# A rewritten constants block, turning of adjacency rows spread into the first run-up, and other buffers for turned rows in a four-layer graph kernel

## The chip, the core and the metric

One core of a Trainium2 chip runs the whole program. The metric is the device time of one execution in microseconds (us). The engines are TensorE (PE, with its weight loads as PEld), VectorE (DVE), ScalarE (ACT), GpSimd (POOL) and SyncE (SP). Each runs its instructions in the order in which the compiled program has them, and they meet through semaphores. All data transfers of this kernel are issued on SP's queue, in order too.

## What is computed

The inputs are `x` (16 elements of 1024 nodes with 64 features), `adj` (16 matrices of 1024 x 1024, zeros and ones) and a node mask. Four layers follow one another, each `x = x + layer(relu(layernorm(x)), adj)`:

```python
# layer 0: thin the neighbour lists, then a weighted sum of quantiles over the neighbours, then an MLP
nb = (adj_ > 0) & (~eye)[None]
m = nb.sum(-1)
rank = jnp.cumsum(nb, axis=-1) - 1
skip = jnp.where(m > T_THRESH, (m + K_DIL - 1) // K_DIL, 1)
removed = nb & do_dil[..., None] & ((rank + 1) % skip[..., None] == 0)
rem = removed | jnp.swapaxes(removed, 1, 2)
...
sv = jnp.sort(vals, axis=2)          # per node and feature, over its valid neighbours
# for tau in 0.25, 0.5, 0.75: linear interpolation between two sorted values, weights 0.25, 0.5, 0.25
out = x + agg
y = relu(out @ W1 + b1) @ W2 + b2
# layer 1: (adj + I) @ h / row sum
# layer 2: attention with 8 heads, a gate from x, and adj added to the logits
# layer 3: adj @ (h @ W3) + b3
```

Layers 1 and 3 multiply by `adj` with the contraction over its columns, so TensorE needs each block of 128 rows of `adj` turned (transposed).

## The kernel before, in words

**Order.** Two generators are interleaved at build time by the loop at the end of the function. `picks()` walks through layer 0; each of its yields hands out an amount of "due" work. `layers()` does all else: first `turned()`, which turns every block of rows of every element, and then, for each element whose layer 0 is done, `rest(b)` (layers 1, 2, 3). Each piece of `layers()` yields its own cost, and the loop lets it go on while something is due. A comparison step of `picks()` yields 0.42 (there are 96 in an element: 8 feature groups, 2 halves of the nodes, 6 order statistics); one turned block costs 0.3; the layers 1 to 3 of one element cost 40.3 together, as much as 96 steps hand out. If the next element's layer 0 isn't done yet, `layers()` yields `None` and what is due is dropped. When `picks()` has ended, `alone` is set and the rest of `layers()` runs without a partner. From the order so written a scheduler in the compiler makes the instruction order of each engine; buffers of one tag are handed out in the written order.

**Constants.** The block from L127 to L352 builds selection matrices and columns on VectorE: identities, bit-reversed indices (`bits_reversed`, `rev`), `at_row` columns, six `sel_q`. It uses a scratch pool that is closed at L389; the main pool `sb` then takes the same memory, so its first load (L394, the node mask) waits for the scratch pool's last user.

**Run-up of element 0.** `ranked(0)` loads and normalises two elements, turns them (`sv`, L956) and stores them (`h_d`). `ranks()` sorts all 1024 values of each of 128 columns in 55 steps of a bitonic network (L577 to L579, three VectorE instructions each), storing the choices (`md`), and stores the sorted values (`vs_d`); then it reads the choices back (`sb`, L597) and runs the 55 steps in reverse on an index row (`rev_d`), four VectorE instructions each (L609 to L612). The result is turned on TensorE (`pr`, L619), copied by ScalarE (`rs`, L622), stored (`rk_d`) and loaded per element (`rk`, L1021). `dilate(0)`, beside it, thins the adjacency in 8 blocks (a scan on VectorE, an Abs on ScalarE, two stores). `background()` deals the two out, two steps of ranking to one of thinning. In the kernel before each of these yields hands out 0.0, so nothing else is interleaved.

**Stages of layer 0.** `stages(el)` loads `rk`, forms the neighbour masks (`neighbours`: two loads `lr` of blocks, TensorE, a ScalarE activation `valid`, 16 times), counts them (`m`, L640), makes the positions of the order statistics (`kq`, six `krow`), and the table of sorted values (`sorted_table`: `u`, `df`, `tab`). For element 0 all of it is written behind `background(0)`; for later elements it lies in the last twelve steps of the element before. `prepare` then makes weights from the ranks (`e`, L705; `cw`), `make` the rank sums (`px`, `cum`, `c1`, `c0`), and `compare` starts with `le` (L819).

**Turning.** `turned()` loads a block of rows (`ad`, L467, three buffers, shared with `dilate` and layer 2), sums it on ScalarE, turns it with eight transposes in two PSUM tiles (`pcols`, L459; copies L462) and stores it (`adjT`, L1096). `turned_rows()` (L1099 to L1102) loads a turned block for layers 1 and 3 into the tag `bt`, which has two buffers. Layer 0's `cum`, `c1` and `c0` use the tag `tb`, six buffers of the same size, which `chunk_cols` already takes for layer 2 once `alone` is set. `weighted()` multiplies a turned block (`two`, L1077), copies it through ScalarE (L1084), and adds its halves on TensorE (`po`, L1086); once alone, both PSUM tiles share one tag of two buffers.

The loop that interleaves:

```python
two, due = layers(), 0.0
for r in picks():
    due += r
    while due > 0.0:
        due -= next(two) or due
alone.append(True)
for _ in two:
    pass
```

Of the kernel before, what the change touches and what calls it, by code (L numbers as in the profile page):

```python
# [8 lines left out]
F32 = mybir.dt.float32  # L9
# [29 lines left out]
def tile_preln_adj_stack(  # L39
# [87 lines left out]
    scr_i = sc("scr_i", (P, 5, P), I32)  # L127
    scr_f = sc("scr_f", (P, 3, P))
    identf = const.tile([P, P], F32, name="identf")
    make_identity(nc, identf)  # L130
    ident = const.tile([P, P], HP, name="ident")
    nc.vector.tensor_copy(ident, identf)

    rev_i = sc("rev_i", (P, C), I32)
    nc.gpsimd.iota(rev_i, pattern=[[1, C]], base=0, channel_multiplier=C)
    rev_a = sc("rev_a", (P, C), I32)
    rev_b = sc("rev_b", (P, C), I32)
    nc.vector.memset(rev_a, 0)
    for b_ in range(N.bit_length() - 1):
        up = N.bit_length() - 2 - 2 * b_  # L140
        nc.vector.tensor_scalar(
            rev_b, rev_i, 1 << b_, abs(up), op0=OP.bitwise_and,
            op1=OP.logical_shift_left if up >= 0 else OP.logical_shift_right,
        )
        nc.vector.tensor_tensor(rev_a, rev_a, rev_b, OP.bitwise_or)
    rev = sc("rev", (P, C), HP)
    nc.vector.tensor_copy(rev, rev_a)
    rev_d = dram.tile([P, C], HP, name="rev_d")
    nc.sync.dma_start(rev_d, rev)
    minus_i = const.tile([P, P], BF, name="minus_i")  # L150
    nc.vector.tensor_scalar(minus_i, identf, -1.0, None, op0=OP.mult)
# [3 lines left out]
    fmp_i = scr_i[:, 0, :]  # L155
    nc.gpsimd.iota(fmp_i, pattern=[[1, P]], base=0, channel_multiplier=-1)
    fmp = scr_f[:, 0, :]
    nc.vector.tensor_copy(fmp, fmp_i)


    step2 = sc("step2")
    nc.vector.scalar_tensor_tensor(step2, fmp, 2.0, identf, op0=OP.is_equal, op1=OP.subtract)
    dif = const.tile([P, 2, P], HP, name="dif")
    nc.vector.tensor_scalar(dif[:, 0, :], step2, -SPAN, None, op0=OP.mult)
    nc.vector.tensor_scalar(dif[:, 1, :], step2, -1.0, None, op0=OP.mult)
    less = const.tile([P, 2, P], HP, name="less")
    nc.vector.tensor_scalar(less[:, 0, :], identf, -2.0, None, op0=OP.mult)
    nc.vector.tensor_scalar(less[:, 1, :], identf, -FINE, None, op0=OP.mult)

    prow_i = scr_i[:, 1, :]  # L170
    nc.gpsimd.iota(prow_i, pattern=[[0, P]], base=0, channel_multiplier=1)
    fcol_i = scr_i[:, 2, :]
    nc.gpsimd.iota(fcol_i, pattern=[[1, P]], base=0, channel_multiplier=0)
    par_i = scr_i[:, 3, :]


    sel_w = const.tile([P, 2, 2 * BKW], HP, name="sel_w")
    nc.vector.tensor_scalar(par_i, prow_i, 1, None, op0=OP.bitwise_and)
    par = const.tile([P, 2], F32, name="par")
    nc.vector.tensor_copy(par[:, 1:2], par_i[:, 0:1])  # L180
    nc.vector.tensor_scalar(par[:, 0:1], par[:, 1:2], -1.0, 1.0, op0=OP.mult, op1=OP.add)
    par_up = const.tile([P, 2], F32, name="par_up")
    nc.vector.tensor_scalar(par_up, par, UP, None, op0=OP.mult)
    for c2 in range(2):
        cols = slice(c2 * BKW, (c2 + 1) * BKW)
        for i, w in enumerate((2.0, 2.0 * FINE)):
            nc.vector.tensor_scalar(
                sel_w[:, i, cols], fcol_i[:, :BKW], 0.0, w, op0=OP.mult, op1=OP.add
            )
            nc.vector.tensor_scalar(sel_w[:, i, cols], sel_w[:, i, cols], par[:, c2 : c2 + 1], None, op0=OP.mult)  # L190

    def bits_reversed(x, bits, n, name):
        r, u = sc(name + "_r", (P, n), I32), sc(name + "_u", (P, n), I32)
        nc.vector.memset(r, 0)
        for i in range(bits):
            up = bits - 1 - 2 * i
            nc.vector.tensor_scalar(
                u, x, 1 << i, abs(up), op0=OP.bitwise_and,
                op1=OP.logical_shift_left if up >= 0 else OP.logical_shift_right,
            )  # L200
            nc.vector.tensor_tensor(r, r, u, OP.bitwise_or)
        return r


    pblk = scr_i[:, 3, :]
    same = scr_f[:, 1, :]
    fblk = scr_i[:, 4, :]
    nc.vector.tensor_scalar(fblk, fcol_i, 4, None, op0=OP.logical_shift_right)
    fpl = sc("fpl", (P, P), I32)
    nc.vector.tensor_scalar(fpl, fcol_i, 15, None, op0=OP.bitwise_and)  # L210
    fplr = bits_reversed(fpl, 4, P, "fpl")
    ppl = sc("ppl", (P, P), I32)
    nc.vector.tensor_scalar(ppl, prow_i, 15, None, op0=OP.bitwise_and)
    pplr = bits_reversed(ppl, 4, P, "ppl")
    nc.vector.tensor_scalar(pblk, prow_i, 4, None, op0=OP.logical_shift_right)
    nc.vector.tensor_tensor(same, pblk, fblk, OP.is_equal)

    to30 = const.tile([P, 2], I32, name="to30")
    field = sc("field", (P, P))
    nc.vector.tensor_scalar(field, pplr, 15.0, None, op0=OP.is_equal)  # L220
    keep = sc("keep", (P, P))
    nc.vector.tensor_scalar(keep, field, -1.0, 1.0, op0=OP.mult, op1=OP.add)
    nc.vector.tensor_scalar(to30[:, 0:1], pplr[:, 0:1], 15.0, keep[:, 0:1], op0=OP.add, op1=OP.mult)
    nc.vector.tensor_scalar(
        to30[:, 1:2], field[:, 0:1], -65536.0 - 1073741824.0, 1073741824.0, op0=OP.mult, op1=OP.add
# [3 lines left out]
    tri = scr_f[:, 2, :]  # L229
    nc.vector.tensor_tensor(tri, pplr, fplr, OP.is_le)  # L230
    nc.vector.tensor_tensor(tri, tri, same, OP.mult)
    nc.vector.tensor_scalar(tri, tri, 0.5, None, op0=OP.mult)
    nc.vector.scalar_tensor_tensor(tri, identf, -40.5, tri, op0=OP.mult, op1=OP.add)
    nc.vector.tensor_tensor(tri, tri, keep, OP.mult)
    nc.vector.tensor_tensor(field, field, same, OP.mult)
    nc.vector.scalar_tensor_tensor(tri, field, 1.0 / KHI, tri, op0=OP.mult, op1=OP.add)
    nc.vector.tensor_scalar(field, fplr, 15.0, -0.5, op0=OP.is_equal, op1=OP.mult)
    nc.vector.tensor_scalar(field, field, 1.0, None, op0=OP.add)
    nth = const.tile([P, P], BF, name="nth")
    nc.vector.tensor_tensor(nth, tri, field, OP.mult)  # L240
# [3 lines left out]
    nc.vector.memset(sel_t, 0.0)  # L244
    for i in range(2):
        nc.vector.tensor_tensor(sel_t[:, i, 8 * i : 8 * i + 8], pblk[:, 0:8], fcol_i[:, 0:8], OP.is_equal)

    sel_c = const.tile([P, 8], F32, name="sel_c")
    nc.vector.tensor_scalar(pblk, prow_i, 7, None, op0=OP.bitwise_and)
    nc.vector.tensor_tensor(sel_c, pblk[:, 0:8], fcol_i[:, 0:8], OP.is_equal)  # L250
# [3 lines left out]
    fbk = sc("fbk", (P, P), I32)  # L254
    nc.vector.tensor_scalar(fbk, fcol_i, 1, None, op0=OP.logical_shift_right)
    pbk = sc("pbk", (P, P), I32)
    nc.vector.tensor_scalar(pbk, prow_i, 63, None, op0=OP.bitwise_and)
    pbkr = bits_reversed(pbk, 6, P, "pbk")
    for e in range(2):
        nc.vector.tensor_tensor(tab_d[:, e, :], fbk, pbkr, OP.is_equal)  # L260
    nc.vector.tensor_scalar(pbkr, pbkr, 1.0, None, op0=OP.add)
    fnx = sc("fnx", (P, P))
    nc.vector.tensor_tensor(fnx, fbk, pbkr, OP.is_equal)
    nc.vector.tensor_scalar(pbk, prow_i, 6, None, op0=OP.logical_shift_right)
    for e in range(2):
        nc.vector.tensor_tensor(tab_d[:, e, :], tab_d[:, e, :], fnx, OP.subtract)
        ph_ = sc("ph_", (P, P))
        nc.vector.tensor_scalar(ph_, pbk, float(e), None, op0=OP.is_equal)
        nc.vector.tensor_tensor(tab_d[:, e, :], tab_d[:, e, :], ph_, OP.mult)
# [4 lines left out]
    nc.vector.memset(none, 0.0)  # L274
    ones = const.tile([P, P], BF, name="ones")
    nc.vector.memset(ones, 1.0)

    k16 = const.tile([P, NBK, 2], HP, name="k16")
    nc.vector.tensor_scalar(
        k16.rearrange("p b s -> p (b s)"), fbk, 16.0, 15.0, op0=OP.mult, op1=OP.add  # L280
    )

    prow = sc("prow", (P, 1))
    nc.vector.tensor_copy(prow, prow_i[:, 0:1])
    off = sc("off", (P, 2))
    bkt = sc("bkt", (P, 1), I32)
    nc.vector.tensor_scalar(bkt, prow_i[:, 0:1], 1, None, op0=OP.logical_shift_right)
    nc.vector.tensor_scalar(off[:, 0:1], bkt, 8.0, -SHIFT, op0=OP.mult, op1=OP.add)
    nc.vector.tensor_scalar(off[:, 1:2], bkt, 0.0, None, op0=OP.is_equal)
    shifts = const.tile([P, 6], F32, name="shifts")  # L290
    nc.vector.tensor_scalar(
        shifts[:, 0:1], off[:, 0:1], -1.0, None, op0=OP.mult
    )
    nc.vector.tensor_scalar(
        shifts[:, 1:2], off[:, 0:1], -SPAN, None, op0=OP.mult
    )
    first = (FIRST - SHIFT) * SPAN / FINE
    rest_ = 8.0 * SPAN / FINE
    nc.vector.tensor_scalar(
        shifts[:, 2:3], off[:, 1:2], first - rest_, rest_, op0=OP.mult, op1=OP.add  # L300
    )
    nc.vector.tensor_scalar(shifts[:, 3:4], shifts[:, 2:3], FINE, None, op0=OP.mult)
    nc.vector.memset(shifts[:, 4:5], -0.5)
    nc.vector.memset(shifts[:, 5:6], 2.0 * (160.0 - FIRST) + 2.0)

    def at_row(dst, terms):

# [203 lines left out]
    def neighbours(left_d, rem_d, t):  # L511
# [3 lines left out]
        for j in range(C):  # L515
# [22 lines left out]
            if j < C - 1:  # L538
                yield None
        yield valid  # L540

    def ranks(V):

# [775 lines left out]
```

## Time and profile before

| what | value |
|---|---|
| runs of the kernel | 12626.17 us median (12620.15 to 12635.34) |
| the profiled execution | 12620.06 us, of which the span of the instructions is 12618.3 |
| VectorE busy | 11557.3 us, 92% of the span |
| TensorE busy | 11271.0 us, 89% |
| ScalarE busy | 9465.7 us, 75% |
| GpSimd busy | 1.4 us, 10 instructions |
| data moved | 908.21 MB, 72 GB/s in the mean |

The profile is of one execution. A group of instructions is named by its line, its engine, its operation and the tiles that it writes and reads (`out<-in`), with partitions x elements. Times of the timeline count from the start of the span. Durations of neighbouring instructions on VectorE and ScalarE overlap a little, so start to start is the better measure of what one costs in a row of many. A line of waits reads: who waited, for whom, total us, how many times, the longest. Waits are inferred from semaphores: of several, the one that came last is named. An engine's share of busy time is a mean over stages that are bound by different things; the stages are therefore read one by one.

### The profile page before, as it was taken

What the parts mean: (1) busy time and instruction counts of PE and PEld (TensorE: products, weight loads), DVE (VectorE), ACT (ScalarE), POOL (GpSimd) and SP (SyncE); (2) the same over time, 40 slices, a digit from 0 to 9 for tenths busy, and PEclk for the clock granted to TensorE, in tenths of its full rate; (3) what the DMA queues carried; (4) which work ended last, traced back from release to release, by engine and by line L of the source; (5) the groups of instructions that cost most, each with busy time, mean ns of one, the idle gap of its engine ahead of it and who ended that gap; (6) DMA issues with size and microseconds to landing.
All of it is one profiled execution on the core that took longest, in us unless ns stands there. A gap on an engine that the chain in (4) does not pass through costs nothing. (4 is left out here: it accounts for less than half of the span.)

```text
span 12618.3 us, 217315 instructions
## 1 busy us (share of the span) xinstructions
PE 11271.0 (89%) x84666; PEld 5355.3 (42%) x84673; DVE 11557.3 (92%) x19682; ACT 9465.7 (75%) x17018; POOL 1.4 (0%) x10
## 2 busy tenths in 40 slices
PE   0888999999899998999989999999999999999988
PEld 0334444444444444444444444444444444444445
DVE  8899989999899999989999899999989999988873
ACT  0897877777777777777877777777777777787866
POOL 0000000000000000000000000000000000000000
PEclk9999999999999999999999999999999999999989
DMA  3672121221212122121211212112121211201011
GB/s 105 219 248 82 56 75 52 71 65 57 71 53 82 55 63 65 54 79 56 71 57 56 78 56 75 54 61 71 55 77 53 72 62 57 88 30 56 31 52 60
DMA packets 521609, 908.21 MB, mean 72 GB/s; under 512 B 240768, under 2 KB 275712, under 8 KB 520576
## 3 DMA queue, kind: packets, MB, share of 16 engines
q1 hardware_dynamic: 520576, 894.31, 21.9%
q8 instruction: 663, 10.86, 0.4%
q14 instruction: 370, 3.03, 0.1%
HBM read 683.38 MB, written 206.57 MB: 71 GB/s over the span
## 5 line engine op out<-in xcount | busy, mean ns | idle before, releaser
L821 DVE TENSOR_TENSOR wa<-le,c 128x2048 f16<-128x2048 f16 x1536 | 1868.8, 1217 | 189.4 <-PE prep L842 127.7
L735 PE MATMUL px<-valid,cw 128*128 128x512 fp8e4 x8192 | 1964.9, 381 | 0.0
L823 DVE TENSOR_TENSOR wb<-le,c 128x2048 f16<-128x2048 f16 x1536 | 1866.9, 1215 | 0.0
L819 DVE TENSOR_TENSOR le<-cum,krow 128x2048 f16<-128x2048 int16 x1536 | 1862.5, 1213 | 2.9 <-ACT cum L406 2.3
L406 ACT ACTIVATE c<-px,shifts 128x512 f16<-128x512 f32 x2048 | 1428.1, 700 | 258.4 <-PE px L762 126.1
L406 ACT ACTIVATE s<-s,nm 128x1024 f32<-128x1024 f32 x1024 | 1171.5, 1147 | 243.1 <-DVE nm L1210 230.1
L735 PEld LDWEIGHTS <-cw 128*128 128x128 f16 x8192 | 799.2, 98 | 1133.1 <-issue 240.1
L459 PE MATMUL pcols<-identf,s 128*128 128x128 f32 x8192 | 1177.8, 281 | 112.5 <-ACT eT L462 49.1
L1201 PE MATMUL sp<-kT,qT 64*128 64x512 f32 x4096 | 1163.5, 641 | 62.8 <-DVE nm L1210 61.3
L869 DVE SCALAR_TENSOR_TENSOR vs<-pz,vs 128x512 f32<-128x512 f32 x1536 | 1047.2, 682 | 148.4 <-PE pz L862 110.4
L459 PEld LDWEIGHTS pcols<-identf,s 128*128 128x128 f32 x8192 | 906.1, 142 | 641.3 <-ACT eT L462 273.4
L849 ACT COPY wi<-prep 128x512 f32<-128x512 f32 x1536 | 913.0, 594 | 347.1 <-PE prep L842 315.6
L842 PE MATMUL val<-le,tab 128*32 128x512 f16 x12288 | 1147.6, 390 | 23.6 <-ACT wi L849 13.1
L462 ACT COPY eT<-pcols 128x512 f32<-128x512 f32 x2048 | 1133.1, 603 | 26.2 <-PE pcols L459 24.8
L406 ACT ACTIVATE high<-px,shifts 128x512 f16<-128x512 f32 x1024 | 712.9, 696 | 582.4 <-PE px L735 577.4
L1224 PE MATMUL ao<-eT,v 128*64 128x128 f32 x16384 | 1071.4, 276 | 21.8 <-ACT eT L462 20.2
L406 ACT ACTIVATE vs<-val 128x512 f32<-128x512 f32 x1536 | 939.5, 612 | 192.1 <-PE val L842 117.5
L1224 PEld LDWEIGHTS ao<-eT,v 128*64 128x64 f32 x16384 | 903.8, 137 | 278.2 <-ACT eT L462 153.7
L842 PE MATMUL prep<-wb,sel_w 128*32 128x512 f16 x6144 | 664.6, 396 | 214.4 <-DVE wb L823 204.7
L1210 DVE CUSTOM_DVE_ANT_0 s<-sp,ad,nm 128x512 f32<-128x512 f32 x1024 | 725.9, 744 | 122.7 <-PE sp L1201 122.6
L857 DVE TENSOR_SCALAR bit<-wi,to 128x512 int32<-128x512 int32 x1536 | 827.0, 538 | 3.6 <-ACT cw L406 2.8
L1210 DVE CUSTOM_DVE_ANT_0 s<-sp,ad 128x512 f32<-128x512 f32 x1024 | 683.3, 682 | 121.7 <-PE sp L1201 112.3
(271 smaller groups left out, 18163.5 us busy)
## 6 DMA issues: line engine op xcount, KB each, us to landing
ad<-in_adj_dram SPq DMA_DIRECT2D x768, 512.0 KB
aT<-adjT SPq DMA_DIRECT2D x256, 512.0 KB
adjT<-aT SPq DMA_DIRECT2D x128, 512.0 KB
md<-sm SPq DMA_DIRECT2D x216, 256.0 KB
sb<-md SPq DMA_DIRECT2D x216, 256.0 KB
rem_d<-rem SPq DMA_DIRECT2D x128, 256.0 KB
left_d<-nb SPq DMA_DIRECT2D x128, 256.0 KB
lr<-left_d SPq DMA_DIRECT2D x256, 128.0 KB
```

Of the source, the lines that this page charges most:

```text
L406: nc.scalar.activation(out_, in_, func, **kw)
L459: nc.tensor.transpose(pt[:, c, :], ad[:, (4 * s + c) * P : (4 * s + c + 1) * P], identf)
L462: nc.scalar.copy(aT[:, 4 * s : 4 * s + 4, :], pt)
L735: yield nc.tensor.matmul(px[pp], w[:, j, :], valid[:, j, :], start=False, stop=j == C - 1, skip_group_check=True,)
L819: nc.vector.tensor_tensor(le, cum, bc(el.krow[q][:, None, hs], [P, 4, 512]), OP.is_lt)
L821: nc.vector.tensor_tensor(wa, le, c0, OP.mult)
L823: last = nc.vector.tensor_tensor(wb, le, c1, OP.mult)
L842: yield nc.tensor.matmul(dst[32 * pp : 32 * pp + 32, :], w[pp], r[pp], start=i == 2, stop=i in (1, 3), tile_position=(0, 32 * pp), skip_gr ...
L869: nc.vector.scalar_tensor_tensor(vs, pz, 80.0, vs, op0=OP.is_equal, op1=OP.mult)
L1201: nc.tensor.matmul(sps[e], qT[e * D : (e + 1) * D, i * P : (i + 1) * P], kT[e * D : (e + 1) * D, hs], start=True, stop=True,)
L1210: nc.vector.tensor_tensor_reduce(ss[e][:, hs], sps[e], ad[:, hs], -1.0, 3.0e38 if t == 0 else nms[e], op0=OP.add, op1=OP.min, accum_out=nm,)
L1224: nc.tensor.matmul(ao[e * D : (e + 1) * D, :], v[:, j, e * D : (e + 1) * D], eTs[e][:, j, :], start=j == 0, stop=j == C - 1, tile_position ...
```

## The change

It has four parts.

1. **Constants.** The block is written anew. Per-partition values that stood 128 wide are now columns of one element; bits of the row number are taken apart once (`ci`, `cf`, `rv`) and reused; index patterns come from more GpSimd `iota`s; copies with a scale (`ident`, `minus_i`, `less`, `dif`, `sel_q`, `mid_w`) go to ScalarE, memsets to GpSimd. The store of `rev_d` is written behind the loads of the weights.
2. **Run-up.** A yield of `background(0)` hands out 0.07 where it handed out 0.0, so `turned()` is interleaved with it. The stages of element 0 join the deal as soon as thinning has ended, beside the second half of the ranking; where they need the sorted values they wait (in the written order) until these are stored. Their tiles `vs`, `u` and `df` come from the tag `a4` for this element, from `q4` for the others.
3. **Ranks of element 0.** They are copied from PSUM straight into the place from which they are used (`own.rk`); the store `rk_d` stays for element 1, and element 0 no longer loads from it.
4. **Turned rows.** Once `alone` is set, `turned_rows()` takes `tb` with its six buffers.

```diff
+    def scaled(name, shape, dt, src, scale):
+        t = const.tile(list(shape), dt, name=name)
+        nc.scalar.activation(t, src, AF.Copy, scale=scale)
+        return t
+
+    ident = scaled("ident", (P, P), HP, identf, 1.0)
...
+    NB = 7
+    ci = sc("ci", (P, NB + 7), I32)
+    for b_ in range(NB):
         nc.vector.tensor_scalar(
-            rev_b, rev_i, 1 << b_, abs(up), op0=OP.bitwise_and,
-            op1=OP.logical_shift_left if up >= 0 else OP.logical_shift_right,
+            ci[:, b_ : b_ + 1], prow_i, b_, 1, op0=OP.logical_shift_right, op1=OP.bitwise_and
         )
...
+    rv = sc("rv", (P, NB))
+    nc.vector.tensor_copy(rv[:, 0:1], odd)
+    for b_ in range(1, NB):
+        nc.vector.scalar_tensor_tensor(
+            rv[:, b_ : b_ + 1], rv[:, b_ - 1 : b_], 2.0, cf[:, b_ : b_ + 1], op0=OP.mult, op1=OP.add
+        )
...
+    nc.vector.tensor_scalar(qs[:, 1:7], identf[:, 0:NQ], -KHI, qs[:, 0:1], op0=OP.mult, op1=OP.add)
     for q in range(NQ):
-        at_row(sel_q[:, q, :], ((q, -KHI), (R_TOP, ones_top * KHI), (R_MID, KHI)))
+        nc.scalar.activation(sel_q[:, q, :], qs[:, q + 1 : q + 2].to_broadcast([P, P]), AF.Copy)
...
-    nc.vector.memset(wproj, 0.0)
+    nc.gpsimd.memset(wproj, 0.0)
...
+    nc.sync.dma_start(rev_d, rev)
     scr.close()
...
+    def place(name):
+        return sb.tile([P, C, D], HP, tag="rk", bufs=2, name=name)
+
...
+        if own is not None:
+            own.rk = place("rk")
+            nc.scalar.copy(own.rk, pt[:, :, :D])
         rs = b2_("rs", (P, C, P), HP)
         nc.scalar.copy(rs, pt)
...
         els[0] = arrive(0)
         for r in background(0):
-            yield 0.0
+            yield 0.07
         for _ in els[0].stages:
             pass
...
             except StopIteration:
                 going.remove(gen)
+                if b == 0 and gen is thinning:
+                    going.append(els[0].stages)
                 continue
...
-        h_d, rk_d, vs_d = pairs[b // 2]
-        el.rk = sb.tile([P, C, D], HP, tag="rk", bufs=2, name="rk")
-        nc.sync.dma_start(el.rk, rk_d[:, :, rows])
-        yield
+        pair = pairs[b // 2]
+        if b:
+            el.rk = place("rk")
+            nc.sync.dma_start(el.rk, pair[2][:, :, rows])
+            yield
...
-        vs = q4("vs")
-        nc.sync.dma_start(vs[rows, :], vs_d[rows, :])
-        table = sorted_table(s, vs)
+        while not pair:
+            yield
+        mine = q4 if b else a4
+        vs = mine("vs")
+        nc.sync.dma_start(vs[rows, :], pair[1][rows, :])
+        table = sorted_table(s, vs, mine)
...
     def turned_rows(b, i, name):
-        aT = sb.tile([P, C, P], F32, tag="bt", bufs=2, name=name)
+        aT = (
+            tb(name, (P, C, P), F32) if alone
+            else sb.tile([P, C, P], F32, tag="bt", bufs=2, name=name)
+        )
         nc.sync.dma_start(aT, adjT[b][i])
         return aT
```

## The prediction

> **What bounds the kernel now.** I read the page's 40 slices first (VectorE at 8 to 9 tenths nearly everywhere, TensorE too), then the busy time by stage, since the change touches only the first element's run-up, its main loop, and the last element's tail.
>
> Busy time by stage; columns: stretch, its length, then busy time (and instructions) of TensorE, its weight loads, VectorE, ScalarE, GpSimd, the granted clock, the DMA share and GB/s.
>
> ```profile
> 24.00:43.00 19.00, 2.42 (x9) 1.75 (x9) 11.94 (x52) 5.41 (x8) 0.00 (x0) 1.00 0.50 139
> 43.00:184.00 141.00, 0.00 (x0) 0.00 (x0) 140.19 (x265) 12.64 (x14) 0.00 (x0) 1.00 0.33 114
> 184.00:287.00 103.00, 1.17 (x9) 0.98 (x10) 92.28 (x225) 0.10 (x1) 0.00 (x0) 1.00 0.27 87
> 287.00:349.00 62.00, 43.15 (x185) 19.50 (x184) 17.56 (x38) 40.77 (x69) 0.00 (x0) 0.89 0.43 115
> 349.00:980.00 631.00, 538.38 (x3730) 246.81 (x3730) 591.14 (x809) 575.77 (x1055) 0.00 (x0) 0.98 0.71 244
> ```
>
> From 43 to 287 us (ranking and thinning of element 0) VectorE alone works; TensorE is empty. From 287 to 349 the roles swap: VectorE is busy 17.56 of 62 us. The next row is element 0's main loop, where VectorE is at 94%. VectorE's waits in the 62 us (total, times, longest):
>
> ```profile
> DVE m L640 <- PE pm L637: 18.4, 1, 18.4
> DVE ve L427 <- ACT sq L406: 15.2, 1, 15.2
> DVE tab L695 <- ACT df L406: 7.5, 1, 7.5
> ```
>
> All wait for work that needed only the thinned masks or the sorted values, both on hand long before 287. Its timeline (start, duration, engine, line):
>
> ```profile
> 286.90 1.01 ACT L622 COPY rs<-pr 128x1024 f16<-128x1024 f16 x1 [119.70 <-PE pr L619]
> ...
> 318.11 0.69 DVE L705 TENSOR_TENSOR e<-k,rk 128x1024 f16<-128x1024 f16 x1
> ...
> 326.30 6.08 ACT L406 ACTIVATE krow<-pkr,shifts 128x512 int16<-128x512 f32 x10
> ...
> 349.11 1.23 DVE L819 TENSOR_TENSOR le<-cum,krow 128x2048 f16<-128x2048 int16 x1 [2.31 <-ACT cum L406]
> ```
>
> The last line is the first comparison of the main loop.
>
> Before 43 us the constants come first. Waits of the DMA queue:
>
> ```profile
> SPq L394 <- DVE q_tau L315: 11.5, 1, 11.5
> SPq L394 <- DMA rev_d<-rev: 2.8, 1, 2.8
> ```
>
> The mask load (L394), ahead of the loads of x, waits for the last constant and goes at 23.80.
>
> **The change, part by part.**
>
> *Constants.* The old block is some 240 VectorE instructions, done at 23.6 us. Counting the new code gives about 88, of which some 20 are 128 wide, plus 13 small ones on ScalarE and some 14 more on GpSimd (0.1 to 0.23 us each in the trace, done by about 5 us, all beside VectorE; the weight load behind the moved memset of wproj waits at most 1 us). What does a narrow instruction cost?
>
> ```profile
> 24.07 0.15 DVE L349 TENSOR_SCALAR rq_f<-rq_f 128x1 f32<-128x1 f32 x1
> 24.26 0.16 DVE L352 TENSOR_TENSOR w_frac<-w_frac,rq_f 128x1 f32<-128x1 f32 x1
> ```
>
> Dependent ones start 0.19 apart; independent ones (14.13, 14.20 us) 0.065. The Trainium skill, "VectorE: DVE Perf Modes", section on the TRN2 errata, says each instruction pays a fixed part (58 cycles plus its elements, at 0.96 GHz), so cutting 128 elements to 1 saves only two thirds: an estimate of 61 ns. By it 88 take 5.4 us; by the dependent row 16.7. They begin at 2.2, so the block ends at 7.6 or 18.9. Chains of different constants mix, so I take 11 us, an end at 13.2. There is a floor anyway: SP issues weight loads until 9.04, rev_d goes to 9.4, and its landing took 2.8, so L394 cannot go before 12.2. L394 moves from 23.8 to 13.2: **-10.5** (ends -5 and -11.6), carried whole to 43, because the chain behind it (landing of x, normalising, turning) is unchanged.
>
> *Hand-over.* Layer 0's stages (neighbour masks, counts, six krow tiles, the table) now go beside the ranking's second half, and the ranks come to SBUF straight from PSUM instead of through HBM. What is left between the ranking's end and the first comparison: transposes 1.03, the copy of 64 columns about 0.6, then the old stretch from the first e (318.11) to 349.11, 31.0 us, less the twelve krow activations, 7.3 us, on ScalarE, its bottleneck there. 1.9 + 31.0 - 7.3 = 26 us. The old distance is 287.2 to 349.1, 62 us: -36. VectorE's part of the stages (m 2x0.69, tab 0.69+1.23+0.69, n and nr 0.54, 0.48, 0.42, 0.42, coef 0.54) is 6.4 us, which idle time covered and which now lengthens a stretch that VectorE bounds: +6.4. Sum **-30** (ends -20 and -36, the latter if the gaps of the ranking's second half, 10.7 us, take it all in).
>
> TensorE might be quicker at the hand-over, having rows to turn before. Sixteen px matmuls took 5.15 us at 320.74, eight took 1.89 at 338.40: warm, four groups would save 2.8 us. The skill's "TensorE: Matmul & The Clock Gate", Part 1, speaks against it: an idle window of about 3.4 us puts the array at half rate. A row every 6 us leaves longer gaps, so by the rule it stays cold; I take nothing.
>
> *Turned rows in the run-up.* The run-up has 1+55+55 yields of ranking, 24 of thinning and 23 of stages: 158 x 0.07 = 11.1, 37 rows at 0.3. Each issues a load and a store of 512 KB on SP, 1.35 us of ScalarE for the row sum, two copies of 0.59, eight transposes. ScalarE and TensorE are free there; VectorE has no part in it. The data fit: in the second half 18 rows x 1.05 MB in 103 us is 183 GB/s, with the 87 of the row above and 41 for the masks 311; element 0 moves 244 at a share of 0.71, so a full share is near 344. What can be late: thinning's rem waits for ScalarE's Abs, which may stand behind a row; the stages' m, tab and krow likewise; and a row's load may stand behind SP's waits for the ranking's buffers (up to 6.8 us each), while ScalarE, which runs in order, waits for that row. The nearest row is element 0's main loop, the same mix: there rem did not wait at all, m 3.8, rev 2.8 us. With the 3.2 us that the ranking already waits for sb, say **+8**. Ends: 0, and 35 us if each of 8 Abs and 6 stage crossings waits for a whole row on ScalarE (2.5 us).
>
> *Element 0's main loop* loses 37 of 128 rows:
>
> ```profile
> L1096 SPq DMA_DIRECT2D adjT<-aT x128: 319/320/1191, 334.3 to 978.2; - x128
> ```
>
> At 0.42/0.3 = 1.4 rows a comparison, the other 91 are through by comparison 64 of 96, and the last third has none. VectorE's waits in this loop:
>
> ```profile
> DVE vs L869 <- PE pz L862: 15.8, 13, 1.9
> DVE wa L821 <- PE val L842: 7.8, 5, 3.5
> DVE wa L821 <- PE prep L842: 6.8, 6, 2.4
> ```
>
> VectorE is idle 14 us from 800 to 975 (7.7 of them in 950 to 975, where rows and next element's stages meet). Rows off TensorE and ScalarE should free most: **-10** (ends 0 and -18). Not more, since VectorE's own work remains. Layers 1 to 3 of element 0 still wait for its layer 0, so later elements keep their work.
>
> *Tail.* Turned rows of the last element get six buffers for two.
>
> ```profile
> 12592.97 1.58 PEld L1077 LDWEIGHTS two<-aT,hid 128*64 128x64 f32 x16
> ...
> 12595.98 1.58 PEld L1077 LDWEIGHTS two<-aT,hid 128*64 128x64 f32 x16
> ```
>
> Rows come 3.01 us apart, also the first two, both loaded 300 us earlier; TensorE waited 0.8 us for these loads in layer 1 and 0.4 in layer 3. The row is a chain through ScalarE and two PSUM buffers: **0** (ends +1, and -9 if an earlier load lets the order overlap 0.6 us a row).
>
> Sum: -10.5 - 30 + 8 - 10 = **-42.5**. The profiled execution took 12620.06 us (span 12618.3); it would take 12577.5. The median of the runs, 12626.17, lies 6 above it, so I predict 12584. Elements 1 to 12 repeat within about 2 us of their kind (starts of the leaving step 743 and 769 apart), so a reshuffled order is worth 5 us or so either way.
>
> **Rivals.** (A) *Partial*: the shared run-up costs its upper bound of 35 us, or rows displace stages and they pile up again: -42.5 + 27 = -15, 12611. For it: SP's in-order queue, already 70 us in waits for L597 before 352. Against: in element 0 the same mix cost VectorE 7 us. (B) *Slower*: rows held by SP's blocked fetches stall ScalarE, the masks come late, and the ranking, which shares its buffers with the masks, stops for each of the rows. It needs more than 68 us to outrun the gain with 25 to spare, 1.8 us for each of 37 rows; at the 3.2 us of the one sb wait it would be 118: +68, 12694. Against: lr loads are few (32) and VectorE's stalls on DMA total 4.2 us. (C) *More*: element 0's waits all go and the tail overlaps: -42.5 - 8 - 9 - 8 (no contention) = -67, 12559. (D) *It doesn't do it*: the stages' instructions still issue last, only constants and rows count: about -15, as A.
>
> **How the numbers follow.** Forecast 0.58, A and D together 0.22, B 0.06, C 0.14. A measurement of this kernel can tell about 0.2%, 25 us, from no change: faster means under 12601. The forecast is faster in nearly all its width, C wholly: 0.74; within, A, D and some of the forecast: 0.20; slower 0.06. The forecast's own range, from its ends, is 12566 to 12604; reaching to C and most of A gives 12556 to 12617.
>
> **What would show it.** L394 issued near 13 us; ranking starting near 32; VectorE's waits for pm and df small; first comparison near 317, not 349; 37 adjT stores before it; none after about comparison 64 of element 0; rows in the tail still 3.0 us apart. Wrong if VectorE waits on sb or lr loads by tens of us between 40 and 290, if the six krow activations still stand behind the ranking's end, or if the element starts drift by more than 5 us each.

## The result, and the profile after

| | before | after |
|---|---|---|
| median of the runs | 12626.17 us (12615.45 to 12635.34) | 12566.01 us (12562.26 to 12573.39) |
| profiled execution (span) | 12620.06 us (12618.3) | 12568.08 us (12566.3) |

The ratio is 0.9954, with a 95% interval of 0.9939 to 0.9968, a gain of 0.5%. (The five runs of the kernel before include the three of the table ahead of the prediction.) The forecast was 12584 in a range of 12556 to 12617. Between the two profiled executions lie 52.0 us, where the prediction's sum had 42.5. A single execution can lie 15 us from the median of its kernel (20 runs of one kernel below: 12590 to 12614 about 12606), so what follows is read stage by stage.

Busy time by stage of the kernel after, columns as before:

```profile
13.00:31.00 18.00, 4.30 (x18) 3.46 (x19) 9.51 (x27) 6.95 (x13) 0.00 (x0) 1.00 0.60 155
31.00:172.00 141.00, 35.42 (x149) 27.90 (x149) 140.00 (x269) 51.81 (x86) 0.00 (x0) 0.53 0.71 257
172.00:275.00 103.00, 56.42 (x262) 33.81 (x261) 87.14 (x211) 55.00 (x98) 0.00 (x0) 0.72 0.89 283
275.00:316.00 41.00, 25.21 (x107) 11.98 (x105) 25.98 (x62) 31.52 (x54) 0.00 (x0) 0.76 0.40 134
316.00:950.00 634.00, 536.39 (x3518) 221.06 (x3516) 603.61 (x828) 518.14 (x926) 0.00 (x0) 0.96 0.54 185
```

The sort takes the 141 us that it took, with VectorE at 140.00, although TensorE and ScalarE now turn rows beside it and the DMA share has gone from 0.33 to 0.71. TensorE is granted 0.53 of its clock there and is busy for 35 of the 141 us.

The timeline of after, at the points shown of before:

```profile
11.53 0.34 SPq L367 DMA_DIRECT2D mk_u<-in_nodemask_dram  x1
...
285.67 0.58 ACT L599 COPY rk<-pr 128x512 f16<-128x512 f16 x1 [2.47 <-PE pr L595]
286.29 1.30 DVE L684 TENSOR_TENSOR e<-k,rk 128x1024 f16<-128x1024 f16 x2 [1.41 <-ACT rk L599]
...
308.46 1.23 DVE L798 TENSOR_TENSOR le<-cum,krow 128x2048 f16<-128x2048 int16 x1 [0.37 <-ACT cum L379]
```

The mask load goes at 11.53, not 23.80, and the first comparison comes at 308.46, not 349.11. The krow activations are gone from the end of the run-up. VectorE's waits from 24 to 310 us:

```profile
DVE ve L400 <- ACT sq L379: 8.6, 2, 7.9
DVE sd L585 <- DMA rev<-rev_d: 4.4, 1, 4.4
DVE tab L674 <- ACT df L379: 3.2, 1, 3.2
DVE sm L553 <- ACT sv L935: 2.7, 1, 2.7
DVE sd L586 <- DMA sb<-md: 2.3, 2, 1.9
```

The wait of 18.4 for `pm` is down to 0.2, and the one for `tab` from 7.5 to 3.2. The one for `ve` does not need masks or sorted values, contrary to the prediction's reading of it: it is the normalising of the next two elements, which stands in VectorE's order there, and 7.9 of its 15.2 us remain. The wait that has grown, from 1.0 to 4.4, is for the index row `rev` at the turn of the ranking (between its sort and its reverse half). The turned rows end at 759.5 us, 39 of them stored before the first comparison:

```profile
L1081 SPq DMA_DIRECT2D adjT<-aT x128: 319/326/795, 31.6 to 759.5; - x128
```

In the tail the rows of layer 3 are 3.01 us apart, as before:

```profile
12537.65 1.98 PE L1062 MATMUL two<-aT,hid 128*64 128x128 f32 x16 [0.68 <-ACT hid L1237]
12540.05 0.69 PE L1071 MATMUL po<-ident,aoT 128*128 128x64 f32 x2 [0.42 <-ACT aoT L1069]
12540.67 1.98 PE L1062 MATMUL two<-aT,hid 128*64 128x128 f32 x16
```

The stages of the profiled executions, in us. The sort is counted to the end of its last `sm`; the "hand-over" is the distance from the ranking's end to the first comparison; the "leaving step" (`o` from `y0`) ends an element's layer 0, and its main loop with it:

| stage | before | after | difference |
|---|---|---|---|
| ranking starts at | 42.82 | 29.77 | -13.05 |
| sort | 142.88 | 143.01 | +0.1 |
| turn, from the sort to the reverse half | 2.23 | 5.58 | +3.35 |
| reverse half | 98.18 | 106.51 | +8.3 |
| hand-over | 63.00 | 23.59 | -39.4 |
| element 0's main loop | 685.2 | 680.0 | -5.2 |
| elements 1 to 15 | 11223.5 | 11221.1 | -2.4 |
| tail after the last leaving step | 360.5 | 356.8 | -3.7 |

### The profile page after: what moved, and what is told of

Same layout as the page of the kernel before. It is cut to its first block, busy times and chain, and to the rows that moved or that the text cites. A ratio compares the mean times of both kernels' runs of the same rounds, so it can differ in the third digit from the quotient of the medians.

```text
span 12566.3 us, 217198 instructions
## 1 busy us (share of the span) xinstructions
PE 11310.1 (90%) x84666; PEld 5369.9 (43%) x84673; DVE 11537.6 (92%) x19522; ACT 9481.0 (75%) x17032; POOL 3.2 (0%) x20
## 5 line engine op out<-in xcount | busy, mean ns | idle before, releaser
L1189 PE MATMUL sp<-kT,qT 64*128 64x512 f32 x4096 | 1162.7, 641 | 63.3 <-DVE nm L1198 58.3
L435 ACT COPY eT<-pcols 128x512 f32<-128x512 f32 x2048 | 1132.8, 603 | 25.9 <-PE pcols L432 24.9
```

What stands on the lines that cost most here:

```text
L435: nc.scalar.copy(aT[:, 4 * s : 4 * s + 4, :], pt)
L1189: nc.tensor.matmul(sps[e], qT[e * D : (e + 1) * D, i * P : (i + 1) * P], kT[e * D : (e + 1) * D, hs], start=True, stop=True,)
```

## The experiments

Each is given with its ratio to the kernel before on the same chip (95% interval) and its median. "The changed kernel" is the basis unless another is named.

**1. The constants alone** (0.9987, 0.9980 to 0.9994; 12605.59 us).

```diff
 # kernel before, all lines up to scr.close() as in the changed kernel
-    nc.sync.dma_start(rev_d, rev)
...
+    nc.sync.dma_start(rev_d, rev)
     scr.close()
```

> The kernel before with the new constants block alone. Theory: the 13.05 us by which the ranking started earlier in the changed kernel come from this block alone and are carried whole to the end, because everything behind it up to the first comparison hangs on one chain. Then the mask load goes near 11.5, the ranking starts near 29.8, its length stays 243.3, the first comparison comes near 336, and the profiled execution takes 12607 (-13). Rival: part of the early start is lost again, since the loads of x and of the adjacency rows now fall together with the loads of the weights; then the ranking starts after 32 or is longer than 245, and the execution takes 12612 or more.

The ranking started at 29.64, took 243.4 and was followed by the old hand-over; the first comparison came at 335.36 (-13.75). The theory held: the early start is carried whole to the first comparison.

**2. Rows only** (0.9994, 0.9985 to 1.0003; 12613.01 us): the kernel before with

```diff
         for r in background(0):
-            yield 0.0
+            yield 0.07
```

> The kernel before with 0.07 handed out by each yield of the run-up and nothing else, which puts some 31 rows beside the ranking. Theory: the rows are nearly free and nearly useless by themselves: ranking 243.3 + 4 = 247, hand-over from its end to the first comparison unchanged at 62 to 64, element 0's main loop 685 - 4 = 681, total 12620 give or take 3. Rival: the rows cost the ranking 20 us or more when they share SP's queue and ScalarE with it: first comparison near 370, total 12635.

Ranking 244.5, hand-over 63.3, main loop 677.1, first comparison 351.64. The 34 rows cost the ranking 1.2 us. So they are nearly free here; what they save can't be told from nothing (the interval reaches 1.0003).

**3. No rows in the run-up** (0.9965, 0.9952 to 0.9978; 12579.03 us).

```diff
-            yield 0.07
+            yield 0.0
```

> The changed kernel with no turned rows in the run-up: its yield hands out 0.0 again, all else stays. Theory: sharing the run-up costs it about 5 us (the wait for the reversal row, the waits for masks) and gives 5 back in element 0, so that it nets nothing: first comparison near 303.5 instead of 308.5, element 0's main loop back at 685, the profiled execution 12568 give or take 3. Rival 1 (as the prediction summed it): the rows cost 8 in the run-up and give 10: first comparison 300.5, main loop 690, total 12570. Rival 2: the sharing is itself a large part of the gain, because TensorE is kept at a higher clock up to the hand-over: then the 23.6 us from the ranking's end to the first comparison become 26 or more without the rows, and the execution takes 12575 or more.

First comparison at 305.08: the rows cost 3.4 us in the run-up (turn 1.2, reverse half 2.7, hand-over -0.7). The hand-over took 24.3 without them, where rival 2 had 26 or more: they don't speed it up by a faster TensorE. Against experiment 1 this run shows the hand-over part by itself: 335.36 to 305.08 is -30.3 (hand-over 62.4 to 24.3, turn +2.1, reverse half +5.6).

Element 0's main loop took 679.3, no longer than with the rows. By pieces, the last 36 of its 96 comparisons took 266.1 before, 264.7 here and 256.7 after, so about 8 us were gained where rows had ended; the first 60 took 419.2, 414.6 and 423.3, with 84 rows in each. The last twelve, where the next element's stages are written, hold most of it:

```profile
879.10:984.40 105.30, 95.87 (x666) 42.42 (x662) 86.74 (x114) 95.28 (x170) 0.00 (x0) 1.00 0.53 165
```

and in after:

```profile
888.20:988.40 100.20, 90.02 (x580) 34.28 (x578) 86.57 (x113) 76.99 (x131) 0.00 (x0) 0.98 0.15 41
```

VectorE's work is the same there (86.7, 86.6); ScalarE loses 18 us of it. The ratios, 0.9965 without the rows and 0.9954 with them, have intervals that overlap: what the sharing is worth in all isn't settled by them. The median without them, 12579.03, is above what the theory and rival 1 had.

**4. The old buffers in the tail** (0.9958, 0.9943 to 0.9973; 12568.56 us): `turned_rows` with tag `bt` only.

```diff
-        aT = (
-            tb(name, (P, C, P), F32) if alone
-            else sb.tile([P, C, P], F32, tag="bt", bufs=2, name=name)
-        )
+        aT = sb.tile([P, C, P], F32, tag="bt", bufs=2, name=name)
```

> The changed kernel with the two old buffers for turned rows of the last element. Theory: the buffers do nothing; the tail from the last leaving step to the end keeps its 356.8 us, rows stay 3.01 us apart, and the 3.7 us by which this tail was shorter than before belong to the clock that TensorE was granted in layer 2, not to the buffers. The profiled execution takes 12568. Rival: the earlier loads move something at the front of the last element's layer 2, and the tail goes back to 360.5: 12572.

The time is unchanged within the interval, but this tail took 360.6, as the rival said. Is it the buffers? In four profiled executions with the new ones (the kernel after, experiments 3, 7 and 8) the tail took 356.8 to 357.4, in four others with them (5, 6, 9 and 10) 360.8 to 361.7. So the new buffers don't make it short. The tails differ where TensorE's clock rises. Up to the rise and behind it, in the kernel after and then here:

```profile
12207.00:12261.60 54.60, 32.39 (x188) 25.70 (x188) 15.28 (x34) 13.34 (x31) 0.00 (x0) 0.50 0.07 20
12261.60:12300.00 38.40, 35.33 (x267) 22.04 (x266) 16.82 (x49) 30.04 (x54) 0.00 (x0) 1.00 0.20 69
```

```profile
12209.00:12275.90 66.90, 44.43 (x220) 32.09 (x221) 16.58 (x38) 16.84 (x36) 0.00 (x0) 0.50 0.21 64
12275.90:12315.00 39.10, 36.46 (x295) 23.06 (x296) 19.62 (x56) 32.41 (x59) 0.00 (x0) 1.00 0.23 81
```

The clock rises 52 us behind the leaving step there and 62.5 here, with the same work in front. The Trainium skill's "TensorE: Matmul & The Clock Gate", Part 1, says that the activity window runs freely, not from the kernel's start, so that the change of clock depends on where in it the work falls. The traces agree. In all of them the stretches of one granted clock last whole multiples of 3.41 us, but for the one that the end cuts off (54.61 us at half rate in the short tails, 64.85 or 68.27 in the long ones). Counted modulo 3.41 us, these steps fall 0.55 to 0.92 us behind the leaving step in the four short tails, and 0.97 to 3.27 us behind it in the eight long ones, the four with the old buffers (before, experiments 1, 2 and 4) among them. So the 3.7 us come from this phase, not from the buffers.

**5. Few rows** (0.9952, 0.9937 to 0.9967; 12562.22 us).

```diff
-        for b in range(B):
+        nc.gpsimd.memset(degree, 1.0)
+        for b in range(4):
             for i in range(C):
...
-        nc.sync.dma_start(aT, adjT[b][i])
+        nc.sync.dma_start(aT, adjT[b % 4][i])
```

> The changed kernel with only elements 0 to 3 turned (32 rows, all within the run-up); later elements read those rows again and their degrees are set to one, so layers 1 and 3 compute something else at the same cost. It shows element 0's main loop with no row beside it. Theory: the rows have no price in that loop; VectorE's own 636 us and the comparison's chain (its waits for pz, val and prep, 25 to 30 us in every run so far) set it, and it takes 676 to 683, as with 91 or with 126 rows. Rival (the prediction's term): rows on TensorE and ScalarE cause these waits; then without any row the loop falls to 665 or less, and VectorE's waits for pz, val and prep to under 12 us together.

Element 0's loop took 665.0. My theory fell, and the rival held almost to the number. The first 84 comparisons and the last twelve:

```profile
312.70:878.40 565.70, 444.73 (x2453) 131.50 (x2453) 548.81 (x756) 311.84 (x508) 0.00 (x0) 0.92 0.11 35
878.40:977.70 99.30, 88.48 (x581) 33.78 (x578) 86.33 (x113) 77.30 (x131) 0.00 (x0) 1.00 0.15 41
```

After's first 84 took 579.7, so its 89 rows cost 14 us, and VectorE's waits for pz, val and prep fall there from 25.4 to 11.7. The last twelve (99.3) are as in after (100.2). It isn't a price by the row, though: in experiment 8, where 52 rows are left for this loop, it took 664.4, as little as with none.

**6. Stages last** (0.9986, 0.9978 to 0.9993; 12605.72 us).

```diff
-                if b == 0 and gen is thinning:
-                    going.append(els[0].stages)
```

> The changed kernel with the stages of element 0 written behind the run-up again, as before; the ranks still come straight from PSUM. Theory: the stages beside the ranking are the hand-over's gain. Then the reverse half falls back from 106.5 to 98 or 99, the distance from the ranking's end to the first comparison grows from 23.6 to 52 to 60 (masks, counts, positions and table once more one after the other), the first comparison comes near 332, and the execution takes 12590. Rival: the trip of the ranks through HBM was what the old 62 us waited for; then this distance stays under 35, the first comparison comes at 305 to 308 and the time is unchanged.

(The run-up then holds 34 rows, since the stages hand none out.) The reverse half went back to 96.9, the hand-over to 63.15, the first comparison to 337.70. VectorE's waits, 270 to 340 us:

```profile
DVE m L619 <- PE pm L616: 18.0, 1, 18.0
DVE ve L400 <- ACT sq L379: 15.4, 1, 15.4
DVE tab L674 <- ACT df L379: 7.6, 1, 7.6
```

They are those of before to 0.4 us, and the hand-over is the old one in full, longer than I had expected, as is the execution (12590 expected). And the ranks:

```profile
275.34 0.59 ACT L599 COPY rk<-pr 128x512 f16<-128x512 f16 x1 [48.32 <-PE pr L595]
...
306.14 0.69 DVE L684 TENSOR_TENSOR e<-k,rk 128x1024 f16<-128x1024 f16 x1
```

They lie in SBUF at 275.9, 30 us before their first use: with the stages behind the ranking, the direct copy is worth nothing.

**7. Ranks through HBM** (0.9962, 0.9947 to 0.9977; 12576.46 us).

```diff
-        for r in ranks(V, els[0] if b == 0 else None):
+        for r in ranks(V, None):
...
         for _ in els[0].stages:
             pass
+        els[0].rk = place("rk")
+        nc.sync.dma_start(els[0].rk, pairs[0][2][:, :, :D])
```

> The changed kernel with element 0's ranks loaded back from HBM again (store of rk_d, then a load) instead of copied from PSUM. Theory: with the stages done the ranks are the last thing waited for, so the store and the load lie open: 23.6 grows by 4 to 6 us, to 28 to 30, first comparison near 313, execution 12573. Rival: ScalarE has other work in these 23.6 us (it is busy 21.8 of 22.5), so the trip hides behind it: under 1 us, no change.

The hand-over grew by 10.2 to 33.8, twice what I expected:

```profile
285.64 1.01 ACT L601 COPY rs<-pr 128x1024 f16<-128x1024 f16 x1 [1.64 <-PE pr L595]
286.68 0.33 SPq L603 DMA_DIRECT2D rk_d<-rs  x1
...
288.89 0.56 SPq L879 DMA_DIRECT2D rk<-rk_d  x1
...
294.90 1.29 DVE L684 TENSOR_TENSOR e<-k,rk 128x1024 f16<-128x1024 f16 x2
```

From the copy's end at 286.65 to the first `e` are 8.3 us, against 0.04 with the direct copy. So the stages alone bring 29.2 of the 39.4 us, the direct copy alone nothing (experiment 6), and 10.2 behind the stages.

**8 and 9. More rows**: 0.14 (1.0033, 1.0020 to 1.0046; 12665.88 us) and 0.10 (0.9979, 0.9970 to 0.9987; 12595.46 us).

```diff
-            yield 0.07
+            yield 0.14
```

> The changed kernel with 0.14 instead of 0.07 handed out by each yield of the run-up, some 74 rows in it instead of 37. Theory: 37 rows cost about 3 us because the transfers still fit (0.71 and 0.87 of the DMA time at 256 and 281 GB/s); twice as many don't: 74 x 1.05 MB and the ranking's own 30 MB at the 330 GB/s or so that full use gives need about 325 us where the ranking takes 255, so the ranking is held up by 40 to 70 us, the first comparison comes at 350 to 380, and element 0's main loop gives nothing back: execution 12610 to 12640. Rival: the scheduler lets the ranking's instructions pass the rows, which then simply run late: first comparison within 5 us of 308, execution 12570.

> The changed kernel with 0.10 handed out in the run-up, some 53 rows in it. 39 rows made the ranking 3 us longer, 76 made it 103 us longer. Theory of a limit: the transfers decide, 53 x 1.05 MB and the ranking's 30 MB in 255 us are 336 GB/s, just at the 320 to 329 that the run with GpSimd's queue reached at full share; so the price is still 10 to 30 us, first comparison at 318 to 335. Rival, a price per row: 2.7 us for each row above 39, first comparison near 345 to 350. Element 0's main loop 670 to 676 in both; execution 12575 to 12590 by the first, 12600 or more by the second.

With 76 rows the first comparison came at 409.72, and the kernel was slower than before (12665.88 us, where the two theories had 12610 to 12640 and 12570); with 55 it came at 340.86, between the two theories. Ranking's start to first comparison took 275.4 with 2 rows, 278.7 with 39, 310.5 with 55, 379.5 with 76: 0.09 us a row, then 2.0, then 3.3. At 0.14, sort and reverse half, and VectorE's waits in them:

```profile
30.00:203.00 173.00, 67.01 (x287) 51.96 (x285) 143.96 (x271) 84.94 (x149) 0.00 (x0) 0.56 0.85 304
203.00:372.00 169.00, 93.54 (x402) 62.85 (x403) 95.90 (x232) 98.36 (x176) 0.00 (x0) 0.62 0.88 295
```

```profile
DVE nb L453 <- DMA ad<-in_adj_dram: 27.3, 7, 5.6
DVE sr L587 <- PE pn L504: 21.9, 9, 4.8
DVE m L619 <- PE pm L616: 18.5, 2, 9.6
DVE sd L585 <- DMA rev<-rev_d: 13.7, 1, 13.7
DVE sd L586 <- DMA sb<-md: 12.3, 5, 4.2
```

Now the ranking itself waits: 94 us in these five. It took 342.3 us with 76 rows, 87 longer than with 39 (the 103 in the text on 0.10 and the 358 in that of experiment 10 are 16 too high), where I had 40 to 70, and 281.5 with 55, 26 longer, where I had 10 to 30. So a limit between 39 and 55 rows is there, and it was priced too low. In the reverse half the transfers hardly speed up with more rows: 283 GB/s with 39, 285 with 55, 295 with 76. The loop gave something back against what I had said: with 52 rows left for it, it took 664.4 instead of 680.0, with 73 it took 673.1:

```profile
409.70:1074.10 664.40, 551.24 (x3448) 205.67 (x3447) 635.02 (x868) 485.19 (x842) 0.00 (x0) 0.97 0.35 119
```

**10. Stores of rows on GpSimd's queue, 0.14** (1.0042, 1.0028 to 1.0055; 12676.13 us).

```diff
-                nc.sync.dma_start(adjT[b][i], chunk_cols(ad, "aT1"))
+                nc.gpsimd.dma_start(adjT[b][i], chunk_cols(ad, "aT1"))
```

> Twice the rows in the run-up (0.14) with the stores of turned rows issued on GpSimd's queue instead of SP's. It asks what made 76 rows cost 101 us where 39 cost 3. Theory of the queue: the DMA engines were at 0.85 to 0.88, not full, while SP stood 132 us in front of stores that wait for ScalarE's last copy of a row, with the loads of ranking and thinning queued behind; with the stores elsewhere the ranking falls from 358 to 300 or less, and the execution from 12666 to 12610 or less. Theory of the transfers: 304 and 295 GB/s is what these transfers can get; the ranking stays at 335 or more, the execution at 12640 or more. In between, both.

The ranking took 315.1, the first comparison came at 388.71, 21 us earlier than in experiment 8: in between. SP's waits in front of row stores (132 us in experiment 8) were gone, and the transfers ran at a higher share:

```profile
30.00:150.00 120.00, 54.07 (x222) 42.55 (x221) 97.70 (x190) 66.75 (x116) 15.00 (x28) 0.52 0.94 329
150.00:290.00 140.00, 67.88 (x316) 50.00 (x317) 98.16 (x211) 71.86 (x131) 15.04 (x29) 0.60 0.93 320
```

So with everything on SP's queue, waiting stores cost some 20 of the 101 us by which 76 rows delay the first comparison. But SP now stood 148 us in front of row loads whose buffers were still being turned, so its order isn't out as a cause of the rest; the transfers, at 0.93 to 0.94, are the other, and I did not part them. The 3.3 us that a row costs between 55 and 76 rows are what its 1.05 MB take at 318 GB/s.

Element 0's loop took 703.2 us, 39 more than in experiment 8, and so the execution is no faster. All of it lies in the first 48 comparisons, which have the 52 rows beside them. ScalarE stands 25.7 us there until a row's store has landed, so that it may fill the buffer again (6.1 us in the whole of experiment 8), and VectorE's wait for pz in the loop is 35.3 us, where it was 7.6:

```profile
ACT aT L435 <- DMA adjT<-aT: 25.7, 13, 5.4
```

That points to stores which free ScalarE's buffers later from GpSimd's queue; no run shows it by itself.

**11. Pipelined rows** (0.9943, 0.9929 to 0.9956; 12549.17 us).

```diff
+    def all_rows(b, name, h, o, cost):
+        late = None
+        for i in range(C):
+            part = weighted(turned_rows(b, i, name), h)
+            if late is not None:
+                halves_added(o[:, i - 1, :], late)
...
-        po = pb("po", (P, D))
+        po = pc_("po", (P, D)) if alone else pb("po", (P, D))
```

> The changed kernel in which the adding of a turned row's halves (po) is written behind the next row's products (two), with po in PSUM buffers of its own once the last element runs alone. It asks what holds the last element's rows 3.01 us apart, where six buffers for two changed nothing. Theory: the chain two, copy, po, copy on TensorE and ScalarE; with the next row's 1.6 us of products in the gap a row takes 1.8 to 2.1, 16 rows save 14 to 19, the tail falls from 357 (361 in the other clock phase) to 340 to 346, and the execution takes 12551. Rival: the rows wait for their loads of 512 KB or for weights; then they stay at 2.8 us or more, tail within 4 us, 12566.

```profile
12537.43 1.09 PE L1062 MATMUL two<-aT,hid 128*64 128x128 f32 x16
12538.45 0.43 PE L1074 MATMUL po<-ident,aoT 128*128 128x64 f32 x2
12538.82 1.09 PE L1062 MATMUL two<-aT,hid 128*64 128x128 f32 x16
```

(Two things change together here, the order and po's buffers; they were not parted.) Rows come 1.39 us apart, closer than the 1.8 to 2.1 that I expected, and the tail took 338.7. The products of a row take 1.09 where they took 1.98. That is the clock (its granted share is the third number from the end); the layer 3 rows of after, then of this kernel, whose share goes from 0.50 to 0.99 at 12537, behind 3.7 us of unbroken products of the first two rows:

```profile
12530.00:12560.00 30.00, 24.90 (x162) 20.52 (x164) 1.21 (x5) 5.08 (x17) 0.00 (x0) 0.50 0.12 36
```

```profile
12530.00:12547.00 17.00, 15.59 (x157) 13.36 (x156) 0.40 (x1) 4.42 (x17) 0.00 (x0) 0.79 0.21 63
```

**12. The last version** (0.9941, 0.9927 to 0.9954; 12545.11 us): experiment 11, and

```diff
+        if own is not None:
+            R = sb.tile([P, N], HP, tag="po", bufs=1, name="rev")
+            nc.sync.dma_start(R, rev_d.rearrange("(o p) c -> o (p c)", o=1).to_broadcast([P, N]))
...
         for _ in make(els[0], 0, 0):
-            yield 0.05
+            yield 0.0
```

> The kernel with pipelined rows at the end (the run before), and two more edits in the run-up: the loop that makes element 0's first sums hands out 0.0 instead of 0.05, so that no turned row is written into the hand-over, where ScalarE was busy 21.8 of 22.5 us, and the index row of the ranking's second half is loaded ahead of the sort into the free tile of layer 1's output. Theory: the wait at the turn of the ranking falls from 5.6 to under 1.5, the hand-over from 23.6 to 20 or 21, the first comparison comes near 301 instead of 308 to 310, and the execution takes 12541 (8 below the run before). Rival: the next thing is as late as the first (the fetched choices at the turn, the positions in the hand-over); then the first comparison comes no more than 2 us earlier and the time stays at 12549.

The rival held: first comparison at 308.77. At the turn another wait took the place of `rev`:

```profile
DVE sd L590 <- DMA sb<-md: 4.9, 1, 4.9
```

and the hand-over without rows took 24.8 (25.0 in experiment 11) although ScalarE's work in it had fallen from the 22 us of after to 18: ScalarE's load doesn't set it. The 4 us to experiment 11 can't be told from nothing. By the ratios both beat the changed kernel by 14 to 16 us; the intervals overlap, but the tail, 339 for 357 us, shows where the gain is.

## Why the prediction was right

The main mechanism was right: element 0's stages run beside the ranking, the hand-over shrinks, and the constants start everything earlier. Each term can be checked against a run.

- **Constants, -10.5:** measured -13.05 to the ranking's start and -13.75 to the first comparison. The 88 VectorE instructions were counted rightly (the old ones are 222, not 240), but the block began at 1.1, not 2.2, and took 8.7 us, not 11. Its timeline shows why:

```profile
7.56 0.14 DVE L275 TENSOR_SCALAR qs<-identf 128x1 f32<-128x1 f32 x1
7.62 0.14 DVE L261 TENSOR_SCALAR shifts<-shifts 128x1 f32<-128x1 f32 x1
7.68 0.14 DVE L265 TENSOR_SCALAR shifts<-nx 128x1 f32<-128x1 f32 x1
7.74 0.15 DVE L276 TENSOR_TENSOR qs<-qs,identf 128x1 f32<-128x1 f32 x1
```

Dependent ones (`qs`) are still 0.18 apart, but the compiled order fills the gap with others, so narrow instructions start every 0.06 us. That is the estimate of 61 ns that the prediction made from the fixed part in the Trainium skill's "VectorE: DVE Perf Modes" (section on the TRN2 errata), not a value midway to the dependent row. The floor of 12.2 for the mask load was 0.7 too high: SP stood 1.3 us for `rev_d`, not 2.8.
- **Hand-over, -30 (-36 and +6.4):** measured -30.3 (-38.1, and +7.7 at the turn and in the reverse half). What the prediction did not see is that of its two edits the stages bring 29.2 by themselves and the direct copy nothing by itself: of two waits only the later one counts. TensorE was at half rate when the hand-over began, as said (granted 0.50 from 289 to 291), but at 0.99 from there to 293.7; the sixteen px products took 4.59 us (5.15 before).
- **Rows in the run-up, +8:** measured +3.4. The term was mis-sized: neither Abs nor masks waited; the wait for `rev` grew by 1.2 and the reverse half by 2.7, with 1.6 of it in the wait for `tab`. The forecast of 311 GB/s for the second half was high (283).
- **Element 0, -10:** measured -5.2. The last store of a row falls at comparison 64, as said. The last 36 comparisons gave 9.3, as the working had it; the first 60, with as many rows as before, took 4.1 longer. In six other kernels with shared rows these took 416.2 to 421.7, in three without 414.6 to 419.2, so the ranges overlap, and whether the 4.1 have a cause stays open. With no rows at all the loop is 20 us shorter than before's (experiment 5), so the end of -18 was about what there is to gain.
- **Tail, 0:** rows stayed 3.01 us apart with six buffers as with two, as predicted. The 3.7 us measured are the phase of TensorE's clock (experiment 4).
- **Elements 1 to 15:** -2.4; over the kernels here they take 11213 to 11231, so this is nothing.

With these sizes the sum is -13.75 - 30.3 + 3.4 - 5.2 - 2.4 - 3.7 = -52.0. The errors of constants and rows, 3.3 and 4.6, point the same way, and the tail added 3.7 by chance; element 0 took 4.8 back. The median fell by 60.2, to the very edge of the forecast's own range (12566 to 12604). The 8 us beyond the sum come from setting the median 6 us above the profiled execution, as it lay before; after, it lies 2 below. So in the number rival C (12559) is nearer than the forecast, 7 us against 18, but its mechanism did not come: the tail did not overlap, and element 0 kept waits.

Rival D (stages still last) is what experiment 6 built: 12605.72, where 12611 was said. Rival B had its mechanism right and its place wrong: masks and fetches that come late stop the ranking, but at 55 rows and above, not at 39.

## What to carry to other kernels

Work put on idle engines beside a bound one can be nearly free up to an amount, and dear behind it; it pays to try several amounts. Here 39 rows cost 0.09 us each, the next 16 cost 2.0 and the 21 behind these 3.3. Two edits on one wait don't add: find which ends last, and what the second is worth once the first is done. More buffers did nothing where a chain between two engines held each row; writing the next row's products into the gap did.

## What was not expected of the hardware

- With a gap of 0.42 us in every 3.01 us TensorE stayed at half its clock through a whole layer (granted 0.50 from 12530 to 12560, busy 24.9 of 30 us by the profile). With the gaps closed, the rows ran at full clock: of the 1.62 us saved per row, 0.89 are the products' own and 0.26 those of `po`. That the gap held the clock down is read from this pair of kernels. The rule of an idle window of about 3.4 us, which the prediction weighed, does not speak of these rows, between which TensorE is never idle for so long; the measurement decides.
- TensorE's granted clock changes on a grid of 3.41 us that does not follow the kernel. Where the last element's start falls on it decides 3.7 us of this kernel's time (experiment 4).
- ScalarE's and TensorE's work and a doubled DMA share beside the sort did not lengthen it: 142.9 us before, 143.0 after.
